# K's seventh block product by seven quarter products too, in a fused two-layer attention kernel

## The chip, the cores and the metric

The kernel runs on one core of one Trainium2 chip. The metric is the device time of one execution in microseconds (us). The record sorts executions into fast and slow ones; all that are quoted here were fast. The share of full TensorE clock that the profile reports as granted is 1.000 before, 0.997 after, and between 0.987 (run 8) and 1.000 in the experiments. In the profile's lines PE is TensorE (matrix products; they land in the memory called PSUM), DVE is VectorE, ACT is ScalarE and POOL is GpSimd; a name like L452 is a line of the kernel's source.

## The reference

Two layers of the same form run one after the other on 8 images of 512 channels and 32 x 32 positions, in fp32: group norm, projections to q, k, v, attention with 8 heads of 64, output projection, residual. Layer 0 has 8 groups, layer 1 has 32.

```python
def layer(x, gn_w, gn_b, qkv_w, qkv_b, proj_w, proj_b, groups):
    xn = group_norm(x, groups) * gn_w + gn_b            # x: (8, 512, 1024)
    qkv = einsum('oc,bcn->bon', qkv_w, xn) + qkv_b
    q, k, v = heads(qkv)                                # 8 heads of 64
    attn = softmax(einsum('bhdi,bhdj->bhij', q, k) / 8)
    out = einsum('bhij,bhdj->bhdi', attn, v)
    return einsum('oc,bcn->bon', proj_w, out) + proj_b + x
```

## The kernel before

A *unit* is one image in one layer; there are 16. In each unit PE first makes Q, K, V of this unit and O (the output projection) of the unit before, then 64 steps of attention. Each of the four projections is a 512x512x1024 product by seven block products where a plain split has eight. From unit 1 on, some of these blocks are themselves made by seven *quarter products*; this nesting is called inner here.

The block that matters is the inner product. Quarters M1, M6 and M7 are accumulated one after the other in the same PSUM place, and ScalarE copies the running sum out after each. So M6 cannot start before ScalarE has copied M1 (in unit 3 of the changed kernel the copy ends at 645.62 us and M6 starts at 645.67).

```python
INNER = {"q": (2, 5, 4, 3), "k": (1, 2, 5, 4, 3), "o": (2, 3, 4)}
ORDER = (1, 2, 3, 6, 5, 4, 7)
...
def inner_products(bank, k, first=False):
    if k not in inner:
        products(bank, k, first, k != 5)          # a block in one piece
        return None
    ...
    dst = {1: one, 6: one, 7: one, 5: two, 2: bank[...], 3: bank[...], 4: bank[...]}
    def step(j):
        nc.tensor.matmul(dst[j], a[j], b[j], start=j in (1, 5) or ..., stop=j not in (1, 6), ...)
        if j in to:                               # 1, 6, 7, 5
            taken.append(nc.scalar.copy(to[j], dst[j]))
```

GpSimd later folds the four copies (two additions of 128x256) and adds them to the outputs (128x512 each). `done()` is called seven times in each of Q, K and V and counts a step `g`; a dictionary says what other work is issued at which step. After K's second block (`g` = 10) the last two heads of the unit before get their division and bias:

```python
def divide_last():
    divide(CC - 1)                                # VectorE, 128x1024
    for h in range(NH):
        add_bias(CC - 1, h)                       # ScalarE, two of 128x512

parts = {3: [lambda: reciprocals(CC - 1)], 10: [divide_last], 17: mixing[:2], 18: mixing[2:3], 19: mixing[3:]}
...                                               # and, in the units with an inner O:
parts[18] += [partial(mix_o, 2)]; parts[19] += [partial(mix_o, 3)]; parts[20] = [partial(mix_o, 4)]
```

## Time and profile before

| | before |
|---|---|
| time, median (lowest to highest) | 3268.86 us (3268.34 to 3270.92) |
| span of the profiled run | 3266.2 us |
| PE / VectorE / ScalarE / GpSimd busy | 3251.4 / 2612.8 / 1623.9 / 1093.3 us |
| PE idle | 14.8 us |

The prediction below shows the lines. One row of a timeline is a run of equal instructions: start, length, engine, source line, output and inputs, shape, count, and in brackets the engine's idle time just before it with what ended it. A PE row is longer than the distance to the next start (two products of 128x256: 0.59 us against 0.43), so the distance from one PE start to the next is taken as the length of what lies between.

### The profile page before, as it was taken

What the parts mean: (1) busy time and instruction counts of PE and PEld (TensorE: products, weight loads), DVE (VectorE), ACT (ScalarE), POOL (GpSimd) and SP (SyncE); (2) the same over time, 40 slices, a digit from 0 to 9 for tenths busy, and PEclk for the clock granted to TensorE, in tenths of its full rate; (3) what the DMA queues carried; (4) which work ended last, traced back from release to release, by engine and by line L of the source; (5) the groups of instructions that cost most, each with busy time, mean ns of one, the idle gap of its engine ahead of it and who ended that gap; (6) DMA issues with size and microseconds to landing.
All of it is one profiled execution on the core that took longest, in us unless ns stands there. A gap on an engine that the chain in (4) does not pass through costs nothing.

```text
span 3266.2 us, 56136 instructions
## 1 busy us (share of the span) xinstructions
PE 3251.4 (100%) x22080; PEld 1838.1 (56%) x22080; DVE 2612.8 (80%) x3364; ACT 1623.9 (50%) x2212; POOL 1093.3 (33%) x1125
## 2 busy tenths in 40 slices
PE   9999999999999999999999999999999999999999
PEld 5455474654746547465574645646556474564743
DVE  5886968879687896878968779687896978969777
ACT  1652726536274462744627446373563735637354
POOL 2051261521616216066160603506125061340610
PEclk9999999999999999999999999999999999999999
DMA  2112120121201212023120111201212012120121
GB/s 94 42 43 78 45 78 28 49 79 43 79 28 43 79 43 85 22 69 114 49 86 27 56 62 54 85 15 42 86 43 85 15 46 82 43 85 15 67 74 48
DMA packets 78394, 188.52 MB, mean 58 GB/s; under 512 B 22064, under 2 KB 27056, under 8 KB 78128
## 3 DMA queue, kind: packets, MB, share of 16 engines
q1 hardware_dynamic: 78128, 184.88, 16.4%
q8 instruction: 178, 2.92, 0.4%
q14 instruction: 88, 0.72, 0.1%
HBM read 144.47 MB, written 38.80 MB: 56 GB/s over the span
## 4 chain that ended last, share of the span: by engine, by line
PE 99%; DVE 0%; DMA 0%; ACT 0%; issue 0%; SPq 0%; DVEq 0%; ACTq 0%
PE a L837 27%; PE s L809 26%; PE s L413 16%; PE a L413 13%; PE a L452 9%; PE s L452 7%; PE a L809 1%; PE s L755 0%; PE a L755 0%; DMA xn<-x_dram 0%; DVE stats L277 0%; PE a L289 0%; ACT p L817 0%; PE s L358 0%; DVE u_q L612 0%
## 5 line engine op out<-in xcount | busy, mean ns | idle before, releaser
L817 ACT ACTIVATE p<-s 128x1024 f32<-128x1024 f32 x976 | 998.2, 1024 | 597.5 <-PE s L809 566.5
L837 PE MATMUL a<-p,v 64*64 64x512 f32 x8192 | 1099.7, 589 | 0.2 <-ACT p L817 0.2
L809 PE MATMUL s<-q,k 64*64 64x512 f32 x7808 | 1058.0, 590 | 0.0
L856 DVE TENSOR_TENSOR acc<-acc,p 128x1024 f32<-128x1024 f32 x768 | 963.8, 1255 | 74.9 <-ACT p L817 21.2
L837 PEld LDWEIGHTS a<-p,v 64*64 64x64 f32 x8192 | 382.6, 131 | 496.8 <-ACT p L817 350.9
L809 PEld LDWEIGHTS s<-q,k 64*64 64x64 f32 x7808 | 383.1, 133 | 433.1 <-issue 426.2
L1053 POOL TENSOR_TENSOR r<-xn 128x256 f32<-128x256 f32 x30 | 52.3, 1744 | 1135.4 <-DVE acc L856 807.2
L854 DVE TENSOR_TENSOR acc<-p,p 128x1024 f32<-128x1024 f32 x128 | 156.5, 1223 | 17.5 <-ACT p L817 17.5
L309 POOL TENSOR_TENSOR y<-var,half 128x4 f32<-128x4 f32 (+1 forms) x17 | 33.2, 1951 | 399.9 <-DVE var L307 399.9
L638 POOL TENSOR_TENSOR k<-k,m_k 128x512 f32<-128x512 f32 x120 | 166.0, 1400 | 0.0
L869 DVE STREAM_TRANSPOSE tr<-acc 128x1024 f32<-128x1024 f32 x128 | 157.9, 1234 | 0.0
L879 DVE TENSOR_REDUCE red<-tr 128x32 f32<-128x1024 f32 x128 | 153.8, 1202 | 0.6
L638 POOL TENSOR_TENSOR q<-q,m_q 128x512 f32<-128x512 f32 x120 | 153.2, 1292 | 0.0
L863 DVE TENSOR_TENSOR ao<-a,tmp 128x512 f32<-128x512 f32 x128 | 87.9, 686 | 65.9 <-ACT tmp L862 65.9
L467 POOL TENSOR_TENSOR m_o<-m_o 128x256 f32<-128x256 f32 x39 | 28.8, 739 | 332.6 <-ACT m_o L457 332.6
L495 ACT COPY p_o<-a 128x1024 f32<-128x1024 f32 x15 | 15.2, 1012 | 244.2 <-PE a L413 244.2
L526 DVE TENSOR_TENSOR u_v<-s,p_v 128x1024 f32<-128x1024 f32 x32 | 39.2, 1224 | 121.2 <-POOL k L635 96.5
L457 ACT COPY m_q<-s 128x256 f32<-128x256 f32 x150 | 55.9, 373 | 146.6 <-PE s L452 132.6
L413 PE MATMUL s<-x_t,s2w 128*128 128x512 f32 x256 | 117.5, 592 | 0.0
L413 PE MATMUL s<-xn,w 128*128 128x512 f32 x256 | 115.5, 594 | 1.8 <-DVE xn L179 1.8
L413 PE MATMUL a<-w,xn 128*128 128x256 f32 x496 | 112.1, 379 | 0.0
L926 ACT ACTIVATE ao<-ao,vec 128x512 f32<-128x512 f32 x128 | 88.5, 715 | 43.4 <-DVE ao L919 43.4
(296 smaller groups left out, 4882.1 us busy)
## 6 DMA issues: line engine op xcount, KB each, us to landing
rb<-drec SPq DMA_DIRECT2D x128, 256.0 KB, 3.9
xn<-mid SPq DMA_DIRECT2D x36, 512.0 KB, 7.5
xn<-x_dram SPq DMA_DIRECT2D x32, 512.0 KB, 7.1
x<-x_dram SPq DMA_DIRECT2D x32, 512.0 KB, 4.6
il<-ilk SPq DMA_DIRECT2D x15, 960.0 KB, 6.3
x<-mid SPq DMA_DIRECT2D x28, 512.0 KB, 4.6
il<-ilq SPq DMA_DIRECT2D x15, 768.0 KB, 4.3
mid<-u_o SPq DMA_DIRECT2D x32, 256.0 KB, 2.1
```

Source lines behind the costliest of these rows:

```text
L413: nc.tensor.matmul(dst, at[:, c, ts(i, P)], moving[:, c, :], start=start and c == 0 and not (tokens and i % 2), stop=stop and c == 1, skip ...
L452: nc.tensor.matmul(dst[j], a[j], b[j], start=j in (1, 5) or first and j in (2, 4), stop=j not in (1, 6), skip_group_check=True,)
L638: w.last[sel].append(add(cols, cols, rest[:, i, :]))
L809: nc.tensor.matmul(bank[e * H : (e + 1) * H, j, :], w.k[pr][j * H : (j + 1) * H, t * P + e * H : t * P + (e + 1) * H], w.q[pr][j * H : (j ...
L817: exp = nc.scalar.activation(p, bank, AF.Exp, scale=SCALE)
L837: nc.tensor.matmul(banks[r][j * H : (j + 1) * H, :], w.v[rows, t, lo : lo + D], p[rows, j, :], start=(t == 0), stop=(t == NT - 1),)
L854: nc.vector.tensor_add(acc, state["first"], p)
L856: nc.vector.tensor_add(acc, acc, p)
L863: i1 = nc.vector.tensor_add(w.ao[pr // 2][:, pr % 2, ts(qh, FD)], banks[1], tmp)
L869: nc.vector.transpose(tr, state["acc"].pop(c))
L879: nc.vector.tensor_reduce(red[:, :, qh, :], state["tr"].rearrange("p j (f i) -> p j f i", i=BL), AX.X, ALU.add)
L926: nc.scalar.activation(cols, cols, AF.Identity, bias=vec[:, units[u][0], VB, pr : pr + 1])
```

## The change

Intent: PE is the bound, and a block in seven quarters takes PE less time than one in one piece (K7: 3.13 us in run 11, 3.43 in run 10), so make K's seventh block that way too. The other parts make room for it (V's first sum no longer waits for a tile that K's sums on GpSimd free; mixings of weights spread differently over unit 7) or take small waits away at the start and in unit 1.

```diff
-    INNER = {"q": (2, 5, 4, 3), "k": (1, 2, 5, 4, 3), "o": (2, 3, 4)}
+    INNER = {"q": (2, 5, 4, 3), "k": (1, 2, 7, 5, 4, 3), "o": (2, 3, 4)}
...
-        products(by, 7, False, False)
+        seventh = inner_products(by, 7)
         u3 = work(*u3_in, "u3")
         summed(1, u3, by, p1)
+        if seventh is not None:
+            fold(seventh)
...                                               # after others(1, 1) and others(1, 0):
+        if seventh is not None:
+            rests(1, 1, seventh)                  # and rests(1, 0, seventh)
...
-                2: (s1, z, ORDER, room_of(tmppool, "tmp")),
+                2: (s1, z, ORDER, room_of(tmppool, "tmp")), 7: (z, s1, ORDER, room_of(tpool, "o4")),
...
+                u2_in=(rbpool, "rb") if w.inner else (trpool, "tr"),      # V's first sum
...
-        def idle_products(n):
+        def idle_products(n, of=gmat.rearrange("p l m -> p (l m)")):
...
-                    for part in {1: made_parts[:4], 7: made_parts[4:]}.get(g, ()):
+                    for part in {1: made_parts[:3], 3: made_parts[3:7], 7: made_parts[7:]}.get(g, ()):
...
-        late = 1 if u == 0 else 0                 # unit 0's group norm steps
-            c -= late
```

(Cut: the mixing of the new right factor on VectorE at `g` = 7 and the new left factors, in the same pattern as the others.)

## The prediction

> **What bounds the kernel now.** I read first the head of the page and its chain of work that ended last.

> ```profile
> span 3266.2 us, 56136 instructions
> PE 3251.4 (100%) x22080; PEld 1838.1 (56%) x22080; DVE 2612.8 (80%) x3364; ACT 1623.9 (50%) x2212; POOL 1093.3 (33%) x1125
> PE 99%; DVE 0%; DMA 0%; ACT 0%; issue 0%; SPq 0%; DVEq 0%; ACTq 0%
> ```

> PE is busy 3251.4 of 3266.2 us and is 99% of the chain. All its idle time is 14.8 us. So a change pays only by taking work from PE or by shortening those 14.8 us, and it costs wherever a slack engine newly makes PE wait. The cores view gives one core at clock 1.000.

> I then read the timeline of one unit (unit 3; a unit is one image in one layer, 16 in all), around the K product that changes:

> ```profile
> 637.03 0.59 PE L452 MATMUL s<-r,w 128*128 128x256 f32 x2
> 637.46 3.60 PE L413 MATMUL s<-xn,w 128*128 128x512 f32 x8
> 640.89 0.59 PE L452 MATMUL s<-x_t,s1w 128*128 128x256 f32 x2
> 641.33 0.59 PE L452 MATMUL a<-r,il 128*128 128x256 f32 x2
> ...
> 637.66 0.37 ACT L457 COPY m_k<-s 128x256 f32<-128x256 f32 x1 [0.49 <-PE s L452]
> 637.93 0.51 ACT L604 ACTIVATE k<-p_k,vec 128x256 f32<-128x256 f32 x1
> 639.78 1.33 ACT L926 ACTIVATE ao<-ao,vec 128x512 f32<-128x512 f32 x2 [1.34 <-DVE ao L919]
> 641.52 0.37 ACT L457 COPY m_k<-s 128x256 f32<-128x256 f32 x1 [0.41 <-PE s L452]
> ...
> 637.23 1.14 DVE L597 SCALAR_TENSOR_TENSOR k<-a,vec,p_k 128x512 f32<-128x512 f32 x2 [1.18 <-PE a L452]
> 638.29 1.45 DVE L919 SCALAR_TENSOR_TENSOR ao<-ao,rb 128x1024 f32<-128x1024 f32 x1
> ```

> The L413 row is K's seventh block product, in one piece: 637.46 to the next start 640.89 is 3.43 us. The L452 rows are quarter products, one each 0.43 us (637.03 to 637.46). What matters most is ScalarE's row at 639.78: two bias additions for the previous unit's last heads stand in its queue between K2's copies and the next product's (641.52). They wait for VectorE's divide (L919, to 639.74), which runs behind L597, which waits for K2's end. Today PE needs nothing of ScalarE in these 3.43 us, so the wait is free.

> [...]
> - [...] ScalarE sits idle 1.34 us ahead of L926.
> - [...] The trace shows gaps to 1.77 us and a granted clock of 1.000; nothing longer is tried here.
> - [...] ScalarE copies M1 out, then PE accumulates M6 on it in the same tile. Hence M6 must wait for that copy.
> - [...] the same 128x256 subtraction takes 0.42 us alone (L213) and 0.83 us beside GpSimd (L566).

> ```profile
> 623.81 0.83 DVE L566 TENSOR_TENSOR k<-xn,k 128x256 f32<-128x256 f32 x1
> 666.25 0.42 DVE L213 TENSOR_TENSOR ro<-ao 128x256 f32<-128x256 f32 x1
> ```

> **The change part by part.**

> *K7 by quarters, PE's work.* Units 1 to 15 swap 3.43 us for 7 × 0.431 = 3.02 us: −0.41 × 15 = **−6.2 us**.

> *K7, ScalarE's order.* The listing of the new instruction order has, on ScalarE: K2's four copies, the k bias, the two L926 biases, then K7's four copies. K7's quarters go in the order M1, M2, M3, M6, M5, M4, M7. Let T be K7's start, 637.46 in this unit.
> - M1 to M3 occupy PE to T + 1.30, and M6 is due then.
> - The biases end at 639.78 + 1.33 = 641.11 = T + 3.65. Nothing ahead of them moves: L597 needs K2's end, as now.
> - M1's copy takes 0.37 us: T + 4.02; a hand-over to PE about 0.03 more. M6 starts at about T + 4.05, a stall of 2.75 us.
> - M6, M5, M4, M7 take 4 × 0.43 = 1.72, and about 0.05 to 0.1 goes to the restart (0.1 more for the first product after a wait at 210.30 below). K7 ends at about T + 5.83.

> That is 5.83 − 3.43 = **+2.4 us a unit**, net of the 0.41 saved. In all 15 units L919 ends 2.27 to 2.30 us after K7's start, so it recurs: 15 × 2.4 = **+36 us**, in place of −6.2. This is the largest term.

> *K7's helpers.* Each unit adds four 0.37 us copies, four 128x256 subtractions on VectorE (2 to 4 us, into 2.4 us of idle time at the end of Q; that product is needed only later), and on GpSimd two folds of 0.73 and four adds of 1.27 us, 6.4 us in sum. GpSimd's part of K then ends near 669 instead of 662 in this unit; its next work, O's, begins near 684. On the path: 0.

> *V's sum in another tile.* Today it waits for GpSimd:

> ```profile
> 657.41 0.72 POOL L635 TENSOR_TENSOR k<-u_k,m_k 128x256 f32<-128x256 f32 x1
> 658.17 1.23 DVE L526 TENSOR_TENSOR u_v<-s,p_v 128x1024 f32<-128x1024 f32 x1 [7.42 <-POOL k L635]
> ```

> This frees a PSUM bank about 0.9 us before PE's next write to it. With 6.4 us more on GpSimd it would have become a PE stall, so the new tile is protection and earns 0 by itself.

> *Idle products on the group matrix (once).*

> ```profile
> 13.59 1.56 PE L358 MATMUL s<-xn 128*128 128x256 f32 x6 [1.45 <-DVE xn L338]
> 14.98 1.45 PE L413 MATMUL a<-xn,w 128*128 128x512 f32 x3
> ```

> Three filler products wait for the normalised xn and keep the first real product to 14.98. On the group matrix they run in the 1.45 us gap, and the real product can start at about 13.55, when its own first piece of xn is ready: **−1.4 us**.

> *Unit 0's steps a chunk sooner (once).*

> ```profile
> 210.30 1.12 PE L413 MATMUL s<-xn,w 128*128 128x512 f32 x2 [1.77 <-DVE xn L179]
> ...
> 198.03 1.75 DVE L179 TENSOR_TENSOR x_t<-xn,x_t 128x1024 f32<-128x1024 f32 x1
> ```

> VectorE's mixing (L179) sits in the last chunk of unit 0's attention, which leaves VectorE behind and PE waits 1.77 us in unit 1. A chunk sooner, that goes: **−1.8 us**. VectorE has room in the earlier chunks.

> *Ten made parts in unit 7 (once).* Four mixings of about 2.5 us now stand on GpSimd in O's stage, ahead of its last adds and store. The first accumulation of attention waits for the slot that this store frees; today GpSimd is done at 1505.72 and the accumulation starts at 1507.86, 2.1 us of slack. Some 6 to 10 us later, with some buffering, I guess **+3 us** (0 to 5).

> Sum: 3268.8 + 36 − 1.4 − 1.8 + 3 = 3304.6; I say **3304**.

> **The rivals.**
> 1. *No stall: the change does what it intends.* Then 3268.8 − 6.2 − 1.4 − 1.8, with 0 to +3 for unit 7: 3259 to 3262. For it: kernels of this sort are usually tuned by trying, and the biases could hide if the divide came earlier. Against it: the order puts the biases ahead of the copies, and each of the three times is read from the trace. It is "the same" still.
> 2. *The stall, and a slower clock after it.* [...] the 1.77 us gap left no mark. If it happened, the 1.72 us of products behind the gap would double: +1.7 × 15 = +26, 3330.
> 3. *VectorE or GpSimd become a bound in K and V.* VectorE is 80% busy, and its subtractions beside GpSimd may double. Then the mixed factor or V's sums come late, perhaps 0.5 to 1 us a unit: 8 to 15 us more, with or without the stall. Against it: the slack counted above, and V's new tile.

> **Range and chances.** The stall's size is uncertain by about 0.3 us a unit (5 us), the single terms by 4 us; a rival 3 of small size adds upward, a shorter stall downward. I take 3295 to 3314 for 8 in 10. Rival 1 has some 0.1. Two per cent faster needs under 3203, far more than PE's idle time and 6.2 us allow: 0.01. Two per cent slower is over 3334, which needs rival 2 or 3 in full: 0.04. Within 2%: 0.95.

> **What would show it right or wrong.** Right: in each of 15 units PE has one new idle of about 2.7 us between M3 and M6 of K7, released by a ScalarE copy, with the two bias additions directly before it; PE's busy time lower by about 6 and its idle time about 40 us more; no 1.77 us gap in unit 1, and the first real product near 13.6. Wrong: no idle in K7 (rival 1), a granted clock below 1.000 (rival 2), or idle before K's second, or V's, products released by VectorE or GpSimd (rival 3). A VectorE divide that starts clearly before T + 0.8 would make the central step fail.

## The result, and the profile after

The changed kernel takes 3320.6 us (3319.34 to 3322.51, four runs) against 3268.86 us. Ratios here are the mean time of one kernel's fast runs over that of the other's of the same rounds, so they are not quite the ratio of the quoted medians: 1.0158, interval 1.014 to 1.0175. That is 51.7 us slower, inside 2%, and above the predicted 3295 to 3314. The intervals are of 95%. The granted clock was 0.997 or 0.998 in all four runs.

The head of the page after, and its chain of work that ended last:

```profile
span 3317.6 us, 56594 instructions
PE 3260.2 (98%) x22170; PEld 1872.7 (56%) x22170; DVE 2683.0 (81%) x3424; ACT 1643.5 (50%) x2272; POOL 1225.2 (37%) x1223
...
PE 81%; POOL 11%; DVE 4%; issue 4%; ACT 0%; DMA 0%; SPq 0%; POOLq 0%; DVEq 0%; ACTq 0%
```

PE's busy time is up by 8.8 us, not down by 6.2 (stretches at half clock, below, add some 8.4 by estimate), and GpSimd, which was not on the chain, is now 11% of it. What PE waited for in the kernel after (total us, times, longest):

```profile
PE a L452 <- ACT m_k L457: 39.2, 15, 2.6
...
PE a L413 <- DVE v L672: 2.9, 9, 0.6
PE a L847 <- ACT p L827: 2.7, 1, 2.7
PE s L413 <- DVE u_v L535: 1.1, 1, 1.1
```

The first row is the predicted stall: 15 times, 2.6 us. The timeline of unit 3 after, PE then ScalarE then VectorE (from L597 on, source lines are 9 or 10 higher than before, so L929 is the divide and L936 the bias):

```profile
641.61 0.59 PE L452 MATMUL a<-xn,w 128*128 128x256 f32 x2
...
642.47 0.60 PE L452 MATMUL s<-xn,il 128*128 128x256 f32 x2
645.67 1.22 PE L452 MATMUL a<-k,il 128*128 128x256 f32 x2 [2.60 <-ACT m_k L457]
646.69 1.06 PE L452 MATMUL s<-k,il 128*128 128x256 f32 x2
...
649.12 0.59 PE L452 MATMUL s<-x_t,s1w 128*128 128x256 f32 x2
...
644.03 1.33 ACT L936 ACTIVATE ao<-ao,vec 128x512 f32<-128x512 f32 x2 [1.44 <-DVE ao L929]
645.27 0.35 ACT L457 COPY m_k<-a 128x256 f32<-128x256 f32 x1
...
642.44 1.54 DVE L929 SCALAR_TENSOR_TENSOR ao<-ao,rb 128x1024 f32<-128x1024 f32 x1
```

K7 starts at T = 641.61. M6 starts at 645.67 = T + 4.06 (predicted T + 4.05), behind the copy, behind the two biases, behind the divide. What was not predicted is the rest: from 645.67 the four quarters take 1.02, 0.85, 0.85 and 0.73 us, start to start, where each took 0.43. The clock has halved: the trace has it at 0.50 from 645.56 to 648.98. The windows view (length, PE busy, ..., granted clock, DMA share, GB/s) shows it for the 3.41 us before and after that point in unit 2, and for unit 14, where it did not happen:

```profile
437.35:440.76 3.41, 1.09 (x5) 0.98 (x6) 0.65 (x2) 1.94 (x4) 3.41 (x4) 1.00 0.34 125
440.76:444.18 3.42, 3.42 (x10) 2.71 (x9) 1.41 (x2) 1.15 (x5) 3.34 (x4) 0.50 0.07 29
...
2908.55:2911.96 3.41, 1.45 (x7) 1.30 (x8) 0.28 (x2) 2.24 (x5) 3.41 (x4) 1.00 0.38 114
2911.96:2915.38 3.42, 3.42 (x18) 3.01 (x17) 1.65 (x3) 1.58 (x5) 3.34 (x5) 1.00 0.10 40
```

Five such half-clock windows of 3.41 us lie in this run, with starts 60, 241, 21 and 161 times 3.413 us apart: four begin in K7, in units 2, 3, 7 and 10, and one lies in unit 7's attention. PE works 16.8 us in the five; at half clock half of that, 8.4 us, is lost, by estimate. Each of the four cost its unit some 1.6 us more than K7's wait alone, partly after K7 (in K7, start to start, against the kernel before: unit 3 +4.08, unit 4, which had none, +2.48).

The single terms came as follows. At the start the first real product moved from 14.98 to 13.66. In unit 1 the 1.77 us wait is gone. Unit 7's wait is there, with the mechanism told in the prediction: VectorE's accumulation now waits for the store of O's output.

```profile
1536.07 1.44 DVE L864 TENSOR_TENSOR acc<-p,p 128x1024 f32<-128x1024 f32 x1 [7.04 <-DMA mid<-p_o]
```

And V waits a little in nine units for its third sum, L672, on VectorE. In unit 13 the subtractions ahead of it (L213, L214) take 1.49 and 1.37 us where they took 0.42 before, while GpSimd is still adding K's pieces beside them:

```profile
2937.81 1.49 DVE L213 TENSOR_TENSOR ro<-ao 128x256 f32<-128x256 f32 x1
2939.33 1.37 DVE L214 TENSOR_TENSOR ro<-ao,ro 128x256 f32<-128x256 f32 x1
```

That GpSimd's work is the cause can be read from the kept traces. In the kernel before, the change and runs 1, 2, 5 and 10, the subtractions of L213 to L216 took 0.41 to 0.43 us in all 763 cases without a GpSimd instruction running beside them, and 0.83 to 1.49 us in all 101 cases with one. In run 2, which is the change without K7's extra work, none is slow.

### The profile page after: what moved, and what is told of

Read it like the earlier page. It is cut to its first block, busy times and chain, and to the rows that moved or that the text cites. A ratio compares the mean times of both kernels' runs of the same rounds, so it can differ in the third digit from the quotient of the medians.

```text
span 3317.6 us, 56594 instructions
## 1 busy us (share of the span) xinstructions
PE 3260.2 (98%) x22170; PEld 1872.7 (56%) x22170; DVE 2683.0 (81%) x3424; ACT 1643.5 (50%) x2272; POOL 1225.2 (37%) x1223
## 4 chain that ended last, share of the span: by engine, by line
PE 81%; POOL 11%; DVE 4%; issue 4%; ACT 0%; DMA 0%; SPq 0%; POOLq 0%; DVEq 0%; ACTq 0%
PE a L847 26%; PE s L819 25%; PE a L413 9%; PE s L413 9%; PE a L452 5%; PE s L452 5%; POOL k L647 2%; POOL q L647 1%; POOL r L575 1%; PE a L819 1%; POOL m_k L466 1%; POOL m_k L465 1%; POOL m_q L466 1%; POOL m_q L465 1%; DVE acc L866 1%
## 5 line engine op out<-in xcount | busy, mean ns | idle before, releaser
L827 ACT ACTIVATE p<-s 128x1024 f32<-128x1024 f32 x976 | 997.5, 1024 | 604.1 <-PE s L819 566.5
L819 PEld LDWEIGHTS s<-q,k 64*64 64x64 f32 x7808 | 391.0, 133 | 425.5 <-issue 418.0
L647 POOL TENSOR_TENSOR k<-k,m_k 128x512 f32<-128x512 f32 x180 | 241.9, 1365 | 0.0
L535 DVE TENSOR_TENSOR u_v<-s,p_v 128x1024 f32<-128x1024 f32 x32 | 39.2, 1224 | 127.7 <-PE s L413 108.9
L457 ACT COPY m_q<-s 128x256 f32<-128x256 f32 x150 | 55.8, 372 | 145.0 <-PE s L452 137.7
L413 PE MATMUL s<-x_t,s2w 128*128 128x512 f32 x256 | 117.5, 592 | 0.0
L413 PE MATMUL a<-w,xn 128*128 128x256 f32 x496 | 112.1, 379 | 0.0
L936 ACT ACTIVATE ao<-ao,vec 128x512 f32<-128x512 f32 x128 | 88.5, 715 | 42.7 <-DVE ao L929 42.7
L457 ACT COPY m_k<-s 128x256 f32<-128x256 f32 x165 | 61.4, 372 | 96.0 <-PE s L452 92.7
```

What stands on the lines that cost most here:

```text
L413: nc.tensor.matmul(dst, at[:, c, ts(i, P)], moving[:, c, :], start=start and c == 0 and not (tokens and i % 2), stop=stop and c == 1, skip ...
L647: w.last[sel].append(add(cols, cols, rest[:, i, :]))
L819: nc.tensor.matmul(bank[e * H : (e + 1) * H, j, :], w.k[pr][j * H : (j + 1) * H, t * P + e * H : t * P + (e + 1) * H], w.q[pr][j * H : (j ...
L827: exp = nc.scalar.activation(p, bank, AF.Exp, scale=SCALE)
```

## The experiments

All give correct results. Each was timed with the kernel before on the same chip.

| run | us, median | ratio to before (interval) |
|---|---|---|
| the change | 3320.6 | 1.0158 (1.014 to 1.0175) |
| 1 last biases after K3 | 3294.32 | 1.0078 (1.0061 to 1.0095) |
| 2 change without K7 | 3268.01 | 0.9997 (0.9988 to 1.0006) |
| 3 V's sum in the old tile | 3363.57 | 1.0288 (1.0271 to 1.0305) |
| 4 unit 7's mixings as before | 3323.44 | 1.0164 (1.0147 to 1.0181) |
| 5 = 1 + O's mixing behind V's sum | 3271.11 | 1.0007 (1.0 to 1.0014) |
| 6 = 5 + unit 7's mixings last | 3269.14 | 1.0002 (0.9993 to 1.0011) |
| 7 quarters of K7 in another order | 3322.18 | 1.0162 (1.0145 to 1.0179) |
| 8 longer wait in K7 | 3360.63 | 1.0282 (1.0265 to 1.0299) |
| 9 = 5 + unit 7 and unit 9, first try | 3268.46 | 0.9999 (0.9991 to 1.0007) |
| 10 = 9 without K7 | 3265.98 | 0.9991 (0.9983 to 1.0) |
| 11 = 5 + unit 7 and unit 9, second try | 3264.92 | 0.999 (0.9981 to 0.9998) |

**1. ScalarE's queue alone.** Only the two biases move; the divide stays.

```diff
-        parts = {3: ..., 10: [divide_last], 17: ...
+        parts = {3: ..., 10: [divide_last], 14: [bias_last], 17: ...   # bias_last: the two add_bias
```

> The changed kernel, with the last heads' two bias additions moved on ScalarE from before K7's copies to after K3's; VectorE's divide stays where it is. Theory A (ScalarE's queue order is the cause and nothing stands behind it): the 2.6 us idle in K7 is gone in all 15 units, and with it the half-clock windows in K7; 3320.6 - 15 x 2.7 - 4 x 1.65 = about 3273 us. Rival B (GpSimd, busy without a break from Q into V, is a bound hidden just behind the stall): K7's idle goes, but V's products now wait, by some 2.4 us more in each unit than the 0.3 us of now; about 3305 us, with new half-clock windows perhaps 3310.

Measured: 3294.32 us, between the two. PE's waits, and unit 3's M6:

```profile
PE a L413 <- DVE v L672: 20.0, 12, 1.7
PE a L452 <- ACT m_o L457: 4.6, 1, 4.6
...
638.66 0.70 PE L452 MATMUL a<-k,il 128*128 128x256 f32 x2
639.20 0.59 PE L452 MATMUL s<-k,il 128*128 128x256 f32 x2
```

K7's wait is gone in all 15 units and M6 follows M3 at once, so the cause of the 39.2 us is shown: two biases ahead of the copies in ScalarE's queue. But V's wait, 0.3 us with the stall, is 1.66 us without it, in 12 units. The 2.6 us stall had given VectorE and GpSimd time. And a wait of 4.6 us appears in unit 7's O.

**2. The change without K7.**

```diff
-    "k": (1, 2, 7, 5, 4, 3)
+    "k": (1, 2, 5, 4, 3)
...                                               # the mixing of its right factor goes too
```

> The changed kernel with K's seventh product in one piece again, all else of the change kept. If K7 explains all of the loss but the single terms: 3268.9 - 1.2 (start) + 0.6 (unit 0) - 1.8 (unit 1) + about 4.5 (unit 7's attention with its half-clock window) = 3271 us, no idle in V. If something else in the change slows it, over 3276.

Measured: 3268.01 us, 3 us below what was expected, since unit 7's wait did not come (its attention is 1.3 us longer than before, not 4.2): the wait needs K7's extra work too. So K7 by quarters is the whole loss (3320.6 - 3268.0 = 52.6 us). The other parts together are within the noise: the ratio's interval holds 1.

**3. V's first sum back in its old tile.**

```diff
-                u2_in=(rbpool, "rb") if w.inner else (trpool, "tr"),
```

> The changed kernel with V's first sum back in its old tile, which K's last sums on GpSimd free. If the new tile is needed: in the changed trace of unit 13 GpSimd frees that tile 5 to 6 us after PE wants the bank again, so PE idles some 5 us in each of 13 to 15 units, mostly long enough for a half-clock window: 3390 to 3420 us. If the tile made no difference: 3321.

Measured: 3363.57 us. The mechanism holds, its size was overstated: in unit 4 VectorE's sum waits 10.68 us for GpSimd and PE 2.23 us for the sum.

```profile
883.60 1.23 DVE L535 TENSOR_TENSOR u_v<-s,p_v 128x1024 f32<-128x1024 f32 x1 [10.68 <-POOL k L644]
...
884.88 3.72 PE L413 MATMUL s<-w,xn 128*128 128x256 f32 x16 [2.23 <-DVE u_v L535]
```

In sum PE waits 34.6 us in 14 units for it, and 14 half-clock windows lie inside the run instead of 5. With K7 by quarters the new tile is needed, as the prediction had it.

**4. Unit 7's mixings placed as before.**

```diff
-   {1: made_parts[:3], 3: made_parts[3:7], 7: made_parts[7:]}
+   {1: made_parts[:4], 7: made_parts[4:]}
```

> The changed kernel with unit 7's ten mixings of weights on GpSimd placed as before (four, then six) instead of three, four, three. If the 2.66 us wait of PE in unit 7's first chunk of attention and the half clock after it come from the four in the middle: about 4.5 us less, 3316 us, with no such wait. If not: 3321.

Measured: 3323.44 us, a miss. The attention's wait is gone, but O now waits 3.02 us for ScalarE's copy (L457) in the same unit, and this run drew seven half-clock windows, not five. The placement only chooses where unit 7 waits.

**5. O's mixing behind V's third sum, on top of 1.**

```diff
-        parts[18] += [partial(mix_o, 2)]; parts[19] += [partial(mix_o, 3)]; parts[20] = [partial(mix_o, 4)]
+        parts[19] = [partial(mix_o, 2)] + parts[19]; parts[20] = [partial(mix_o, 3)]; parts[21] = [partial(mix_o, 4)]
```

> The first experiment (last biases after K3) with VectorE's four subtractions for O's second product (L213 to L216) put behind V's third sum (L672) instead of ahead of it, the two later mixings one step later too. In the first experiment these four took 1.48, 0.83, 0.94 and 1.48 us beside GpSimd, against 0.41 alone, and PE waited 1.66 us in 12 units for L672 behind them. Theory (V's wait is VectorE slowed by GpSimd's longer chain): the V waits go, 15 x 1.75 = -26 us, and only unit 7's wait of 4.6 us remains: 3268 us. Rival (GpSimd itself, or PSUM, is what V waits for): no change, 3294.

Measured: 3271.11 us. V's third sum now waits only for PE, and the slowed subtractions stand behind it, where nobody waits for them:

```profile
2896.85 1.22 DVE L672 TENSOR_TENSOR v<-a,u_v 128x1024 f32<-128x1024 f32 x1 [0.66 <-PE a L413]
2897.99 0.98 DVE L213 TENSOR_TENSOR ro<-ao 128x256 f32<-128x256 f32 x1
2899.01 1.37 DVE L214 TENSOR_TENSOR ro<-ao,ro 128x256 f32<-128x256 f32 x1
```

All 12 waits on L672 are gone, so V's wait was VectorE's order and pace, not GpSimd's own end nor PSUM. After the start, the waits of over 1 us that are left are those of O in unit 7 (4.6 us) and for V's second sum in unit 9 (1.3 us).

**6. Unit 7's ten mixings all after O's last step**, on top of 5: `{7: made_parts}`.

> As the run before, with all ten of unit 7's weight mixings on GpSimd after O's last step. If unit 7's wait (ScalarE's copy of M1 behind GpSimd's mixings) was theirs: a further -4.6 and -1.7 for its half-clock window, 3262 us, under both kernels. If the wait only moves to the attention that follows: 3266 to 3268.

Measured: 3269.14 us. The 4.6 us wait in O went and one of 3.47 us in the next attention came, with its half-clock window: the wait moved.

**7. Another order of K7's quarters, in the changed kernel.**

```diff
-   7: (z, s1, ORDER, ...)
+   7: (z, s1, (1, 5, 2, 3, 4, 6, 7), ...)
```

> The changed kernel with K7's quarters in the order M1, M5, M2, M3, M4, M6, M7. PE now has 2.15 us of work before it needs ScalarE's copy, so the main idle shrinks to about 1.8 us, with one of 0.5 before M7: K7 shorter by some 0.3 us. If the clock halves because one idle stretch fills most of a window of 3.4 us: no half-clock window in K7, 3320.6 - 15 x 0.3 - 4 x 1.65 = 3309.5. If the halving comes from anything else in K7, the number of them stays and it is 3316.

**8. A longer wait in K7.** One more VectorE instruction ahead of the last divide, in the changed kernel.

```diff
+            nc.vector.tensor_scalar(same, same, 1.0, 0.0, ALU.mult, ALU.add)   # 128x1024, values unchanged
             divide(CC - 1)
```

> The changed kernel with one more VectorE instruction (128x1024 times 1 in place, 0.6 to 1.2 us) ahead of the last divide. The idle in K7 grows by its length, to 3.2 to 3.8 us. If the clock's halving depends on how much of a 3.4 us window the idle fills, nearly all 15 units get a half-clock window instead of 4: 3320.6 + 15 x 0.9 + 10 x 1.65 = about 3350. If it were chance independent of the gap: 3334.

Measured: 3360.63 us. The wait grew from 2.6 to 3.74 us, by 1.14 (the 0.6 to 1.2 of the expectation was an estimate of mine), and all 15 units got a half-clock window. In 11 of them a second one followed at once, as in unit 14:

```profile
2941.07:2944.48 3.41, 1.02 (x5) 0.56 (x3) 3.05 (x5) 0.83 (x3) 3.41 (x3) 1.00 0.10 23
2944.48:2947.90 3.42, 2.07 (x5) 1.71 (x6) 0.00 (x0) 1.67 (x4) 3.37 (x4) 0.50 0.34 131
2947.90:2951.31 3.41, 3.41 (x10) 2.69 (x9) 1.41 (x2) 1.12 (x3) 3.38 (x4) 0.50 0.00 0
```

Against the change, PE is idle 12.8 us longer (16.9 in K7, less in V and unit 7), and by the estimate above the half clock costs 36.9 us where it cost 8.4. That makes 41.3 us; the spans differ by 40.8. That PE waits for VectorE's divide by way of ScalarE's queue is shown a second time, from the other side.

To see what the half clock goes with in these runs, nine traces (the change, and runs 1 and 3 to 9) were cut into windows of 3.413 us on the grid that each trace's half-clock windows mark (each of those five in the change is 3.413 us long), and PE's idle time was summed in each. Of the windows that the trace records at full clock (its clock records begin 7.27 us into the change's span), the table has those with at least 1.2 us of it (none with less was followed by half clock); of those at half clock, all 63:

| PE idle in a window of 3.413 us | next window at full clock | at half clock |
|---|---|---|
| at full clock itself: 1.20 to 1.69 us | 53 | 0 |
| at full clock itself: 1.70 to 2.00 us | 13 | 7 |
| at full clock itself: over 2.00 us | 0 | 42 |
| at half clock itself: up to 0.55 us | 49 | 0 |
| at half clock itself: 0.59 us and more | 0 | 14 |

In the change all 15 waits in K7 (2.60 to 2.63 us) lie across a border of two windows. Four have 2.03 to 2.49 us on one side of it: a half-clock window followed, and the unit took some 1.6 us more. The other eleven have at most 1.95 us on one side, and none followed. A half-clock window with up to 0.55 us of idle time was the last one in 49 of 49 cases; one with 0.59 us and more was followed by a second in 14 of 14, as where run 8's long wait reaches into it (in unit 14, 2.07 us busy of 3.42). Where nothing else disturbs them, the change's units repeat about every 204.9 us, which is 60.03 windows, so neighbouring units fall nearly alike: units 2 and 3 both had it, 11 to 15 had not.

**9, 10 and 11. Is K7 by quarters worth anything with every wait out of the way?** Run 9 is run 5 with unit 7's mixings as `{3: made_parts[:3], 7: made_parts[3:]}` and unit 9's mixing of the projection weights at step 18 instead of 16. Run 10 is run 9 without K7 in `INNER` and the mixing of its factor. Run 11 has `{3: made_parts[:4], 7: made_parts[4:]}` and step 20.

> The fifth experiment (last biases after K3, mixing for O's second product behind V's third sum), with unit 7's weight mixings as three after O's third step and seven after its last (GpSimd idled 4.27 us before O's second fold in the sixth experiment), and unit 9's mixing of the next projection weights two steps later on VectorE (PE waited 1.26 us there). Nothing should be left of the change but its saving: from the sixth experiment 3269.1 - 3.5 - 1.7 (unit 7's wait and half-clock window) - 1.3 (unit 9) = 3262.6 us. If unit 7's wait only moves again: 3267.

> The kernel beside this one with K's seventh product in one piece. The difference of the two is K7's own worth with every wait of the change out of the way: PE saves 0.41 us less 0.1 for slightly later helpers in each of 15 units, in the sixth experiment 0.3 each, so 4.5 us: about 3267 us. If it is nearer the 6.2 us of the count of products, 3269.

> The ninth experiment with unit 9's mixing of the projection weights at the last but one step of V (VectorE stood idle 3.23 us there, and the first of the mixed weights is needed 3.4 us after V), and unit 7's weight mixings as four and six instead of three and seven. If unit 9's wait (2.72 us and a half-clock window) and unit 7's (2.2 us in sum) go: 3268.5 - 4.3 - 1.6 = 3262.6 us, some 3.4 us under the same kernel without K7 by quarters. If either only moves: 3265 to 3267.

Measured: run 9 3268.46 us, a miss: step 18 put four mixings of 1.1 to 1.75 us ahead of V's third sum in unit 9, and PE waited 2.72 us there instead of 1.26, with a half-clock window. Run 10 3265.98 us. Run 11 3264.92 us: unit 9's wait is gone, but unit 7's attention is 2.4 us longer than in run 10 (waits of 0.62 us for ScalarE, L827, and of 0.74 and 1.09 us at the group norm's small products, L289). Run 11 is the fastest of all, 0.1% under the kernel before; its lead of 1.1 us over run 10 is within the spread of the runs. Of the runs without the stall, 9 and 10 are the only pair that differs in K7 alone, and there K7 by quarters loses 2.5 us by unit 9's wait; run 11 has no twin without K7. Stage by stage the worth is clear: K7 takes 3.13 us in each of the 15 units of run 11 where run 10 takes 3.43. It saves 0.3 us, not 0.41, because M6 waits 0.11 us for M1's copy even when ScalarE is free: in run 1's lines above, 638.66 to 639.20 is 0.54 where the others take 0.43.

## Why the prediction was right or wrong

- **PE's saving, -6.2 us:** right as a count, too high as a time; 0.3 a unit (runs 10 and 11), about -4.5.
- **K7, ScalarE's order, +36 us net:** right in mechanism and size. M6 at T + 4.06 against T + 4.05; the hand-over to PE, which I put at 0.03 us by estimate, took 0.05 (645.62 to 645.67). Start to start, unit 4 has 847.54 to 853.45 = 5.91 us for K7 where it had 3.43: +2.48 against +2.4, 37 us in 15 units.
- **The first failed step, the clock's term: "the 1.77 us gap left no mark."** The granted clock was 1.000 in that run; that a gap of 2.75 us leaves none either was an estimate of mine that no trace showed, and by it I put the clock's term at zero. In the nine traces of the table, summed idle time from 1.7 to 2.0 us in a window at full clock was followed by a window at half clock in 7 of 20 cases, and over 2.0 us in 42 of 42. In the profiled run that made 4 x 1.6 after K7's waits and 1.7 in unit 7, some 8 us. Rival 2, set at 15 x 1.7, was right in kind (two quarters took 0.85 us for 0.43) and too large in size.
- **The second failed step, K7's helpers, "On the path: 0":** of about the same size. Nine waits on L672 and one on L535 made V 0.54 to 0.57 us longer in eight units, 0.85 in unit 4 and 1.32 in unit 9, in sum 6.6 us. The units with a half-clock window in K7 had no such wait. I had counted GpSimd's end against O's need (its 6.4 us are 6.5 by the terms given), and left out that VectorE's subtractions in V take longer beside its longer chain (0.83 to 1.49 us, against 0.41 to 0.43 alone). That is rival 3, at a little under its 8 to 15 us. With the stall gone this becomes the next bound (run 1).
- **V's sum in another tile, 0 by itself but needed:** right (run 3).
- **Idle products, -1.4, and unit 0's steps, -1.8:** the stage up to unit 0's attention is 1.2 us shorter, unit 1 gains about 1.8; unit 0's attention is 0.6 longer, with a wait of 0.44 us at the group norm's product (L289) that was not there. In sum -2.4, predicted -3.2.
- **Unit 7, +3 (0 to 5):** the wait is 2.66 us by the predicted path; with the half clock behind it the attention of unit 7 is 4.2 us longer.

Sum: 37 + 6.4 + 6.6 + 4.2 - 2.4 = 51.8 us, against 51.4 between the two spans. Taken off one at a time, the clock's 8.1 us would leave 3312.5 us of the 3320.6, and V's 6.6 us 3314.0. Shown by experiment: ScalarE's order as the cause of K7's wait (1), V's wait as VectorE's order (5), slowed by GpSimd's work for K7 (2), the need of the new tile (3), the clock's dependence on idle time (7, 8). Not shown by an experiment of its own: what unit 0 lost, and what decides between full and half clock from 1.7 to 2.0 us.

## What to carry to other kernels

When a change puts a hand-over (a PSUM copy that the next product needs) on an engine that was slack, read that engine's queue in program order: an unrelated instruction ahead of the copy, which waits for a third engine, becomes a stall of the bound engine (here 2.6 us in each of 15 units). Taking that stall away pays only until the next wait that it covered, here 26 of 52 us, so look for what ran in its shade before counting the gain. In this kernel a PE stall of 2.6 to 2.7 us cost up to 1.7 us more than its length, depending on where it fell, and one of 3.74 us up to some 2.8, by estimate.
